# A recurrence of 30 steps on one core: eps inside the aggregated variance, another set of groups transposed by DMA, one PSUM copy moved to VectorE, and a new order of work inside a slot

## The chip, the cores and the metric

The kernel runs on one core of a Trainium2 chip. The metric is the device time of one launch in microseconds (us). Engine names are those of the profile: PE is TensorE (PEld its weight loads), DVE is VectorE, ACT is ScalarE, POOL is GpSimd, SP is SyncE, which here only issues DMAs.

## The reference, cut to what matters

The network has two layers over 3327 nodes with 256 features: a graph attention and a mixture of experts, then a second graph attention and a recurrent feed-forward part. Only that last part, the recurrence, is touched. It computes, 30 times in a row and row by row:

```python
def step(h, _):
    h = h + 0.01 * jnp.tanh(h)
    h = h * jax.nn.sigmoid(h)
    h = _layernorm(h, ln_w, ln_b)          # (h - mu) * rsqrt(var + 1e-5) * w + bias
    h = jnp.einsum('bsc,dc->bsd', h, W) + b
    return (h, None)
x, _ = jax.lax.scan(step, x, None, length=30)
```

It starts from a layernorm of `x`, and its result is added to `x`. Every row is independent of the others, so the steps of different rows can run beside each other.

## The kernel before, in words

The rows lie as 26 tiles of 128 rows in the on-chip tensor `x` (128 partitions x 26 x 256, float32). The recurrence works on seven *groups*: groups 0 to 5 have four tiles each, group 6 has two. A group in a step is one `Group` object, numbered `at` from 0 to 209; `at % 7` is the group, `at // 7` the step. The state is kept times 100 (`S`), and the subtraction of the mean and the weights of the normalization are folded into the 256 x 256 matrix `wc` and the row `bb`, so only the reciprocal standard deviation is needed for each row, and it is applied after the product.

One group in one step goes through these pieces, with their lines in the kernel before:

- `tanh` (L1109, ACT) writes `th`; `add` (L1112, POOL) adds the state to it; `silu` (L1116, ACT) writes `z`.
- `measure` (DVE): for each tile `bn_stats` over 256 values (L1121), which leaves six numbers [...], then `bn_aggr` (L1124), which makes mean and variance of them, then one small instruction that adds eps (L1127). `invert` (L1132, POOL) raises it to the power -1/2.
- The product needs `z` transposed. A group that is not `away` is turned on the core: `turn_here` issues two PE transposes of 128x128 per tile (L1142), and ACT copies them out of PSUM for two tiles at a time (L1144). A group that is `away` is turned by DMA: `send_away` lets ACT split the 4-byte values into 2-byte halves (L1152, once for two tiles) and SP issue a store of them to DRAM (L1154); `take_back` lets SP issue transposing DMAs that bring them back (L1164, one for two tiles). `AWAY` (L1091) lists the groups that are turned by DMA, from `at` = 2 on.
- `product` (L1177, PE): two matmuls per tile with `wc`, each of which the profile records as two. `evict` (L1187, DVE): one instruction per tile multiplies by the reciprocal deviation, adds `bb` and writes the state. In the last step it also loads the kept `x` (`old`, L1194, SP), adds it (L1195, DVE) and stores the result (L77, SP).

The loop at L1209 is the schedule. In each pass, a *slot*, it issues pieces of seven different groups: `tanh` for the group six ahead of the product, `add` and `silu` five ahead, `send_away` four ahead, `measure` and the turning three ahead, `invert` one ahead, the product, and the eviction of the group one behind. Nearly all of these are bound to that order on their engine (`keep_in_program_order`), so each engine's queue is the order of the lines in the loop: on ACT the split copies, then `tanh`, `silu` and the copies out of PSUM; on DVE the eviction, then `measure`; on POOL `invert`, then `add`; on PE the product, then the transposes; on SP the sends, then the eviction's DMAs in the last step, then the takes. The engines wait for each other only where data or a buffer demands it. Buffers: three `th`, four `z`, two `zT`, two product tiles in PSUM, three tiles for the halves and five for what comes back, four places in DRAM.

The matmuls of the second attention (L286) run until about 1080 us; the first steps of the recurrence are begun beside them.

Of the kernel before, what the change touches and what calls it, by code (L numbers as in the profile page):

```python
# [11 lines left out]
F32 = mybir.dt.float32  # L12
# [5 lines left out]
ALU = mybir.AluOpType  # L18
# [3 lines left out]
P = 128  # L22
ALPHA = 0.2
EPS = 1e-5
N_STEPS = 30
S = 100.0
G = 4
# [4 lines left out]
def gat_moe_gat_recurrent_ffn(ctx: ExitStack, tc: tile.TileContext, a: dict, out: bass.AP):  # L32
    nc = tc.nc
    N, D = a["x"].shape
# [65 lines left out]
    neg_half = const.tile([P, MOST], F32, name="neg_half")  # L100
# [902 lines left out]
        for name, bufs in (("th", 3), ("z", 4), ("zT", 2))  # L1003
    }
    narrow = ctx.enter_context(tc.tile_pool(name="narrow", bufs=8))
    ps = ctx.enter_context(tc.tile_pool(name="ps2", bufs=2, space=PSUM))
    with ExitStack() as st:
        keep = st.enter_context(tc.tile_pool(name="keep2", bufs=1))
# [71 lines left out]
    with ExitStack() as st:  # L1080
# [7 lines left out]
        spaces = [space[:, i * G * D : (i + 1) * G * D] for i in range(8)]  # L1088
        room_parts, room_back = cycle(spaces[:3]), cycle(spaces[3:])

        AWAY = (0, 1, 3, 5)  # L1091
        COUNT = len(groups)
        LAST = N_STEPS * COUNT

        class Group:

            def __init__(self, at):
# [3 lines left out]
                self.hs = x[:, self.ts[0] : self.ts[0] + self.n, :]  # L1101
                self.away = at % COUNT in AWAY and at > 1

# [12 lines left out]
                self.put(nc.scalar.activation(self.z, self.th, AF.Silu, scale=1.0 / S))  # L1116

            def measure(self):
                stats = narrow.tile([P, G, 6], F32, name="stats")
                for j in range(self.n):  # L1120
                    self.put(nc.vector.bn_stats(stats[:, j, :], self.z[:, j, :]))  # L1121
                self.v = narrow.tile([P, G, 2], F32, name="v")
                for j in range(self.n):
                    self.put(nc.vector.bn_aggr(self.v[:, j, :], stats[:, j, :]))  # L1124
                self.r = narrow.tile([P, G], F32, name="rr")
                self.put(
                    nc.vector.tensor_scalar(self.r[:, : self.n], self.v[:, : self.n, 1], EPS, None, op0=ALU.add)  # L1127
                )

            def invert(self):  # L1130
                r = self.r[:, : self.n]
                self.put(nc.gpsimd.tensor_tensor(r, r, neg_half[:, : self.n], ALU.pow))  # L1132

            def turn_here(self):
                pool = next(turns)
                zT = steps["zT"].tile([P, G, KD, P], F32, name="zT")
                for c in range(self.n // 2):
                    pt = pool.tile([P, 2, KD, P], F32, name="bank")
                    for j in range(2):
                        for k in range(KD):  # L1140
                            (tc.keep_in_program_order if self.at > 1 else lambda ins: ins)(
                                nc.tensor.transpose(pt[:, j, k, :], self.z[:, 2 * c + j, k * P : (k + 1) * P], ident)  # L1142
                            )
                    self.put(nc.scalar.copy(zT[:, 2 * c : 2 * c + 2, :, :], pt))  # L1144
                self.zT = lambda j, k: zT[:, j, k, :]

            def send_away(self):
# [52 lines left out]
        live = {}  # L1200

        def on(at, *what):
            if 0 <= at < LAST:
                if at not in live:
                    live[at] = Group(at)
                for w in what:
                    w(live[at])

        for at in range(-6, LAST + 2):  # L1209
            on(at + 4, lambda g: g.away and g.send_away())  # L1210
            on(at - 1, Group.evict)
            live.pop(at - 1, None)
            on(at + 6, Group.tanh)
            on(at + 1, Group.invert)
            on(at + 5, Group.add)
            on(at + 3, Group.measure)
            on(at, Group.product)
            on(at + 3, lambda g: g.away and g.take_back())
            on(at + 5, Group.silu)
            on(at + 3, lambda g: g.away or g.turn_here())  # L1220


# [47 lines left out]
```

## Time and profile before

| | |
|---|---|
| median of 3 runs | 1831.34 us (1829.67 to 1831.44) |
| the profiled execution | 1831.93 us |
| its span, first to last instruction | 1830.2 us |
| mean granted TensorE clock | 0.996 |
| the recurrence's products (L1177) | from 1083.0 to 1822.4 us |
| busy in the span | PE 1778.3, DVE 1318.7, ACT 1229.7, POOL 914.0 us |
| costliest groups of the recurrence (us busy, mean ns of one) | products on DMA-turned tiles 422.2, 379; products on PE-turned tiles 281.0, 379; `add` 464.8, 2213; evictions 325.0, 477; `bn_stats` 274.0, 411; split copies 235.2, 1044; `tanh` 209.1, 996; `silu` 207.1, 986; `invert` 206.7, 984 |
| issued by DMA | 236 stores `apart<-adjT` of 256 KB, 236 transposes `adjT<-apart` |

How to read it: times of one instruction overlap the next one on the same engine, so the mean length of a matmul is not what it takes of PE's stream; for that the starts of neighbours are compared. A view of the profile names an instruction by its line and by the tensor it writes and reads (`po<-wc,adjT` is a product on what the DMA brought back, since those buffers share the memory of the adjacency matrix `adjT`). The profiled execution's own time stands beside its span because a sum of durations belongs to that execution, not to the median.

### The profile page before, as it was taken

To read this page: it belongs to the slowest core of one execution; us is meant where nothing else is said; L and a number is where in the kernel's file an instruction comes from. 1 tells how busy PE (TensorE), PEld (TensorE's weight loads), DVE (VectorE), ACT (ScalarE), POOL (GpSimd) and SP (SyncE) were. 2 spreads that over 40 slices of the span, in tenths; PEclk is the share of its full clock that TensorE was granted. 3 is DMA by queue.
4 is the path that set the end of the run, shared out by engine and by line. 5 is a ranking of instruction groups with operands and counts; after the bars stand their busy time and mean duration, and the time that the engine had idled before them with its cause. 6 is when DMAs were issued, how large, how long until landed. Compare 5 with 4: busy or idle time off the path is not lost.

```text
span 1830.2 us, 32461 instructions
## 1 busy us (share of the span) xinstructions
PE 1778.3 (97%) x10896; PEld 1622.7 (89%) x10896; DVE 1318.7 (72%) x4039; ACT 1229.7 (67%) x1587; POOL 914.0 (50%) x702
## 2 busy tenths in 40 slices
PE   6999999999999999799999999999999999999998
PEld 6999999898999999688888878888888888888887
DVE  6888888853222222657676679999999999999998
ACT  2877667642122121456666579999999999999994
POOL 3011212155454542101111028898889889888984
PEclk9999999999999999899999999999999999999999
DMA  8897360257696876400000037777777777767777
GB/s 174 119 125 85 73 102 15 67 168 207 218 264 186 220 203 164 154 15 16 18 22 14 12 91 175 175 166 175 167 168 179 168 177 168 173 166 169 179 168 224
DMA packets 454531, 252.98 MB, mean 138 GB/s; under 512 B 327493, under 2 KB 426620, under 8 KB 454362
## 3 DMA queue, kind: packets, MB, share of 16 engines
q1 hardware_dynamic: 436226, 212.51, 47.1%
q0 software_dynamic: 13456, 33.60, 10.8%
q10 hardware_dynamic: 4680, 4.76, 0.8%
q8 instruction: 89, 1.46, 0.3%
q14 instruction: 80, 0.66, 0.1%
HBM read 168.19 MB, written 97.20 MB: 145 GB/s over the span
## 4 chain that ended last, share of the span: by engine, by line
PE 54%; DVE 4%; DMA 1%; issue 0%; ACT 0%; POOL 0%; SPq 0%; ACTq 0%; DVEq 0%; POOLq 0%
PE po L1177 35%; PE acc L286 14%; PE bank L1142 4%; DVE pT L281 1%; PE acc L163 1%; DMA old<-kept 1%; DVE x L1187 0%; DVE x L1027 0%; DVE stats L1121 0%; DMA given<-wh,to 0%; DVE x L1195 0%; DMA zT<-given 0%; DVE st L116 0%; POOL rstd L121 0%; DVE low L1061 0%
## 5 line engine op out<-in xcount | busy, mean ns | idle before, releaser
L276 ACT ACTIVATE e<-rb,minus,full 128x384 f32<-128x384 f32 (+3 forms) x494 | 399.2, 823 | 168.0 <-DVE pT L281 147.1
L1112 POOL TENSOR_TENSOR th<-th,x 128x1024 f32<-128x1024 f32 (+1 forms) x210 | 464.8, 2213 | 94.3 <-ACT th L1109 86.6
L281 DVE SCALAR_TENSOR_TENSOR pT<-e,part,adjT 128x384 f32<-128x384 f32 (+3 forms) x494 | 383.4, 782 | 118.3 <-PE acc L286 102.3
L1177 PE MATMUL po<-wc,adjT 128*128 128x256 f32 x1888 | 422.2, 379 | 0.0
L1177 PEld LDWEIGHTS po<-wc,adjT 128*128 128x128 f32 x1888 | 356.4, 190 | 47.6 <-DVE x L1187 0.3
L1187 DVE SCALAR_TENSOR_TENSOR x<-po,rr,bb 128x256 f32<-128x256 f32 x780 | 325.0, 477 | 61.6 <-PE po L1177 61.1
L286 PE MATMUL acc<-wh,pT 128*128 128x129 f32 x2704 | 310.7, 276 | 2.1 <-DVE pT L281 2.1
L286 PEld LDWEIGHTS acc<-wh,pT 128*128 128x128 f32 x2704 | 305.4, 192 | 3.2 <-DVE pT L281 2.5
L286 PE MATMUL acc<-s_wh,pT 128*128 128x257 f32 x1352 | 295.5, 381 | 4.0 <-DVE pT L281 4.0
L286 PEld LDWEIGHTS acc<-s_wh,pT 128*128 128x128 f32 x1352 | 255.8, 190 | 43.1 <-DVE pT L281 7.4
L1177 PE MATMUL po<-wc,zT 128*128 128x256 f32 x1232 | 281.0, 379 | 0.6 <-DVE x L1187 0.6
L1121 DVE BATCH_NORM_STATS2 stats<-z 128x6 f32<-128x256 f32 x780 | 274.0, 411 | 1.4 <-ACT z L1116 1.4
L1177 PEld LDWEIGHTS po<-wc,zT 128*128 128x128 f32 x1232 | 229.2, 190 | 29.6 <-issue 0.9
L1152 ACT COPY adjT<-z 128x1024 int16<-128x1024 int16 x236 | 235.2, 1044 | 4.8 <-DVE pT L281 2.0
L121 POOL TENSOR_TENSOR rstd<-ve,neg_half 128x4 f32<-128x4 f32 (+3 forms) x28 | 31.9, 1141 | 411.5 <-DVE ve L119 313.0
L1109 ACT ACTIVATE th<-x 128x1024 f32<-128x1024 f32 (+1 forms) x210 | 209.1, 996 | 28.9 <-DVE x L1187 23.8
L1132 POOL TENSOR_TENSOR rr<-rr,neg_half 128x4 f32<-128x4 f32 (+1 forms) x210 | 206.7, 984 | 26.4 <-DVE rr L1127 26.3
L1116 ACT ACTIVATE z<-th 128x1024 f32<-128x1024 f32 (+1 forms) x210 | 207.1, 986 | 8.3 <-POOL th L1112 2.3
L931 ACT ACTIVATE e<-bank 128x512 f32<-128x512 f32 x61 | 36.4, 597 | 241.0 <-issue 183.2
L939 DVE TENSOR_TENSOR pT<-e,bank 128x512 f32<-128x512 f32 x61 | 41.9, 687 | 190.8 <-PE bank L881 160.7
L903 POOL DMA_INDIRECT given<-wh,to x61 | 61.1, 1001 | 119.2 <-DVE wh L902 102.8
L594 POOL DMA_INDIRECT lists<-pair,ati x52 | 63.5, 1221 | 107.5 <-DVE ati L581 49.3
(202 smaller groups left out, 1731.9 us busy)
## 6 DMA issues: line engine op xcount, KB each, us to landing
wh<-in_w_dram SPq DMA_DIRECT2D x120, 512.0 KB
apart<-adjT SPq DMA_DIRECT2D x236, 256.0 KB
first_set<-in_w_dram SPq DMA_DIRECT2D x63, 512.0 KB
in_bytes<-in_adj_dram POOLq DMA_DIRECT2D x3, 2496.0 KB
asked<-e POOLq DMA_DIRECT2D x42, 128.0 KB
adjT<-apart SPq DMA_TRANSPOSE x236
x<-in_x_dram SPq DMA_DIRECT2D x6, 512.0 KB
kept<-x SPq DMA_DIRECT2D x8, 384.0 KB
```

What stands on the lines that cost most here:

```text
L276: nc.scalar.activation(e[:, : n * P], rb[:, : n * P], AF.Relu, scale=sc.full[:, j, h : h + 1], bias=sc.minus[:, j, h : h + 1],)
L281: masked = nc.vector.scalar_tensor_tensor(pT[:, : n * P], e[:, : n * P], sc.part[:, j, h : h + 1], adjT[:, j // 2, ts[0] * P : (ts[-1] + 1 ...
L286: nc.tensor.matmul(po[c], lhsT=pT[:, c * P : (c + 1) * P], rhs=wh[:, j, h, :], start=(j == 0 and c % per_bank == 0), stop=(j == NT - 1), s ...
L1109: self.put(nc.scalar.activation(self.th, self.hs, AF.Tanh, scale=1.0 / S))
L1112: self.put(nc.gpsimd.tensor_tensor(self.th, self.th, self.hs, ALU.add))
L1116: self.put(nc.scalar.activation(self.z, self.th, AF.Silu, scale=1.0 / S))
L1121: self.put(nc.vector.bn_stats(stats[:, j, :], self.z[:, j, :]))
L1132: self.put(nc.gpsimd.tensor_tensor(r, r, neg_half[:, : self.n], ALU.pow))
L1142: nc.tensor.transpose(pt[:, j, k, :], self.z[:, 2 * c + j, k * P : (k + 1) * P], ident)
L1152: self.put(nc.scalar.copy(parts[:, c : c + 2], halves[:, c : c + 2]))
L1177: nc.tensor.matmul(self.po[:, j, :], lhsT=self.zT(j, k), rhs=wc[:, k, :], start=(k == 0), stop=(k == KD - 1),)
L1187: nc.vector.scalar_tensor_tensor(self.hs[:, j, :], self.po[:, j, :], self.r[:, j : j + 1], bb, op0=ALU.mult, op1=ALU.add)
```

## The change

The change does four things in the recurrence.

1. **eps.** The statistics of eight groups get one tensor that is written once, `measures`, with nine numbers for each tile: the six of `bn_stats` and a third entry that is constant (count 0, mean 0, sum of squares EPS x 256). `bn_aggr` reads all nine, so its variance contains eps. The DVE instruction that added eps is gone, and POOL's power reads the aggregated variance directly.
2. **Which groups are turned by DMA.** `AWAY` is (0, 2, 4, 5, 6) instead of (0, 1, 3, 5): 18 tiles instead of 16. On PE remain groups 1 and 3 instead of 2, 4 and 6: 8 tiles instead of 10. Groups 4, 5, 6 and the next step's 0 follow each other.
3. **One copy out of PSUM.** Of group 3's two copies, the first is done by DVE instead of ACT.
4. **The order of a slot.** `tanh` and `invert` come ahead of `send_away`. The eviction belongs to the product's own group and stands behind the product and ahead of `measure`, where it was of the group one behind and stood near the head. The loop ends two passes earlier, and the number of pieces is the same.

On the queues that means: ACT has `tanh` before the split copies; DVE has the eviction of group s before `measure` of s+3 where it had `measure` of s+4 after it; on SP, in the last step, the eviction's load and store of group s stand ahead of the take of s+3, where those of s-1 did. POOL's and PE's order within a slot is the same.

```diff
+    measures = ctx.enter_context(tc.tile_pool(name="measures", bufs=1)).tile([P, 8, G, 9], F32, name="stats")
+    nc.vector.memset(measures[:, :, :, 6:8], 0.0)
+    nc.vector.memset(measures[:, :, :, 8:9], EPS * D)
...
-        AWAY = (0, 1, 3, 5)
+        AWAY = (0, 2, 4, 5, 6)
...
             def measure(self):
-                stats = narrow.tile([P, G, 6], F32, name="stats")
+                stats = measures[:, self.at % 8]
                 for j in range(self.n):
-                    self.put(nc.vector.bn_stats(stats[:, j, :], self.z[:, j, :]))
+                    self.put(nc.vector.bn_stats(stats[:, j, :6], self.z[:, j, :]))
                 self.v = narrow.tile([P, G, 2], F32, name="v")
                 for j in range(self.n):
                     self.put(nc.vector.bn_aggr(self.v[:, j, :], stats[:, j, :]))
+
+            def invert(self):
                 self.r = narrow.tile([P, G], F32, name="rr")
                 self.put(
-                    nc.vector.tensor_scalar(self.r[:, : self.n], self.v[:, : self.n, 1], EPS, None, op0=ALU.add)
-                )
-
-            def invert(self):
-                r = self.r[:, : self.n]
-                self.put(nc.gpsimd.tensor_tensor(r, r, neg_half[:, : self.n], ALU.pow))
+                    nc.gpsimd.tensor_tensor(
+                        self.r[:, : self.n], self.v[:, : self.n, 1], neg_half[:, : self.n], ALU.pow
+                    )
+                )
...
-                    self.put(nc.scalar.copy(zT[:, 2 * c : 2 * c + 2, :, :], pt))
+                    copied = nc.vector.tensor_copy if (self.at % COUNT, c) == (3, 0) else nc.scalar.copy
+                    self.put(copied(zT[:, 2 * c : 2 * c + 2, :, :], pt))
...
-        for at in range(-6, LAST + 2):
-            on(at + 4, lambda g: g.away and g.send_away())
-            on(at - 1, Group.evict)
-            live.pop(at - 1, None)
+        for at in range(-6, LAST):
             on(at + 6, Group.tanh)
             on(at + 1, Group.invert)
+            on(at + 4, lambda g: g.away and g.send_away())
             on(at + 5, Group.add)
+            on(at, Group.product, Group.evict)
             on(at + 3, Group.measure)
-            on(at, Group.product)
             on(at + 3, lambda g: g.away and g.take_back())
             on(at + 5, Group.silu)
             on(at + 3, lambda g: g.away or g.turn_here())
+            live.pop(at, None)
```

## The prediction

> **What bounds the kernel now.** I read the slices first, then the stages, the waits and the order of time. In the page's totals and its 40 slices (one digit is the busy tenth of a slice) the part that the diff touches, the recurrence, is the last 40%:
>
> ```profile
> PE 1778.3 (97%) x10896; PEld 1622.7 (89%) x10896; DVE 1318.7 (72%) x4039; ACT 1229.7 (67%) x1587; POOL 914.0 (50%) x702
> ...
> PE   6999999999999999799999999999999999999998
> ```
>
> All engines look busy there, so the view by stages (us; then PE, PEld, DVE, ACT, POOL, clock, DMA share, GB/s) and the waits from 1050 us on decide:
>
> ```profile
> 1400.00:1600.00 200.00, 200.00 (x1009) 176.97 (x1009) 181.91 (x693) 189.10 (x220) 178.32 (x114) 1.00 0.76 172
> ```
> ```profile
> POOL th L1112 <- ACT th L1109: 78.8, 61, 2.9
> DVE x L1187 <- PE po L1177: 61.1, 89, 1.8
> ...
> ACT th L1109 <- DVE x L1187: 23.8, 29, 0.8
> ...
> PE po L1177 <- DVE x L1187: 0.6, 1, 0.6
> ```
>
> DVE waits for PE, ACT for DVE, POOL for ACT; PE waits 0.6 us in all. The chain starts at PE. The order of time gives PE's prices and the slack of the DMA path (start, length):
>
> ```profile
> 1501.84 7.07 PE L1177 MATMUL po<-wc,adjT 128*128 128x256 f32 x32
> ...
> 1508.75 1.04 PE L1142 MATMUL bank<-ident,z 128*128 128x128 f32 x8
> ...
> 1509.62 3.62 PE L1177 MATMUL po<-wc,zT 128*128 128x256 f32 x16
> ...
> 1512.96 1.99 ACT L1152 COPY adjT<-z 128x1024 int16<-128x1024 int16 x2
> ...
> 1513.35 1.66 DVE L1187 SCALAR_TENSOR_TENSOR x<-po,rr,bb 128x256 f32<-128x256 f32 x4 [0.88 <-PE po L1177]
> 1514.03 6.01 SPq L1154 DMA_DIRECT2D apart<-adjT  x4
> ...
> 1515.04 1.06 ACT L1109 ACTIVATE th<-x 128x1024 f32<-128x1024 f32 x1
> ...
> 1520.13 5.31 SPq L1164 DMA_TRANSPOSE adjT<-apart  x4
> ...
> 1526.48 3.83 PE L1177 MATMUL po<-wc,adjT 128*128 128x256 f32 x17
> ```
>
> 16 product records cost (7.07-3.62) = 3.45 us, so 0.2156 us each from start to start; 8 transposes cost 1509.62-1508.75 = 0.87, so 0.109 each. A step has 104 records and 20 transposes: 22.42 + 2.18 = 24.60 us, and the trace's step (group 0 from 1501.84 to 1526.48) is 24.64. **PE issues without a gap: a step is the sum of its matmuls.**
>
> [...] busy is 100%, weight loads are 177 of 200 us, and only the start-to-start times show that nothing is left. [...] Here its row says 273, but it takes 109 of PE's stream, which is the price used. [...] `take_back` waits on the landing of `send_away`, with everything behind it in SP's queue; the trace shows it, in SP's own waits from 1400 to 1600 us:
>
> ```profile
> SPq L1164 <- DMA apart<-adjT: 18.9, 16, 2.2
> ```
>
> **The change, part by part.** P0 to P6 are the products of groups 0 to 6 (P6 half as long), "turn" the transposes on PE.
>
> *Groups turned by DMA.* Before, groups 2, 4, 6 (10 tiles, 20 transposes a step) stay on PE; after, 1 and 3 (8 tiles, 16). In all 600+16 transposes become 480+8, 128 fewer. A step falls by 4 x 0.109 = 0.44 to 24.20 us. Before the first product, group 2's eight go (16 transposes stand at 1081.23, the product at 1083.00): 0.87. So up to the last step: 0.87 + 29 x 0.436 = **13.5 us less**, if PE stays without gaps.
>
> *ACT.* One int16 copy a step more (nine for eight, 0.95 from start to start), two PSUM copies fewer (five become four, one goes to DVE; 0.47 each): about 0. ACT stays at 189.1/200 x 24.64 = 23.3 us, now of 24.2.
>
> *DVE.* Seven eps additions go (172 ns rows): -1.2 us. One PSUM copy comes: between ACT's 576 ns row and the 687 of the DVE row with a PSUM operand of that size (L939), I take 0.66. `bn_aggr` on nine entries for six is not in the trace: between 0 and half of its 66 ns step, 0 to 0.9 us; I take 0.1. Net -0.4 of 22.4: off the path. The copy sits in the slot of P0, 3.45 + 0.87 = 4.33 long, where DVE has 3.24 + 0.66 = 3.9; without that cover it costs at most 0.6. Two memsets at the layer's start run while DVE is idle.
>
> *The order of a slot.* Eviction of s still precedes `tanh` of s+7, but three waits are new or longer.
> (a) On ACT, `tanh` now stands ahead of the copies. Above, the copies of group 0 ran at 1512.96, before the `tanh` that had to wait for the eviction's end at 1515.01; they would now start at 1516.0, 3 us later, with silu, PSUM copy and SP's send behind them.
> (b) On DVE, `measure` of s+3 now follows the eviction of s. So POOL's power of s+3, which stands ahead of the addition of s+7, waits for `bn_aggr`, some 3.3 us after the eviction starts. POOL has 0.99 + 2.32 = 3.3 us of work in a slot of 3.45, so it keeps up; the addition comes 1.5 to 2 us later than `tanh` would allow.
> (c) On SP, groups 4, 5, 6, 0 go in a row. From P0 = 0 (P4 14.7, P5 18.1, P6 22.5, next P0 24.2), with evictions starting 0.28 after a product and ending 1.66 later, sends come at about 4.2/5.2 (group 4), 8.4/9.4 (5), 12.2 (6), 15.2/16.2 (0), 22.1/23.1 (2). Takes follow, each behind the next group's send: 9.7, 12.6, 16.5, 17.8, 25.0. A take of two transposes needs 2 x 1.25 us on SP, and I give 2.6 us from a transpose's issue to its landing (packets of the pair issued from 1503.82 end near 1507.9). First halves land at 12.3, 15.2, 19.1, 20.7, 27.6: 2.4, 2.9, 3.4, 3.5 and 4.4 us ahead of their products. Before, by the same rule, the nearest was group 0: 1520.13 + 2.6, 3.8 ahead of its product at 1526.48. Thinner now, but positive, so I cost it at nothing. SP issues 9 x (0.37+1.25) = 14.6 us a step (13.0 before); DMA share goes from 0.76 to 0.76 x 9/8 x 24.64/24.20 = 0.87.
>
> *The ends.* The head shows no new stall: the send of group 2 comes before the last attention result, and its second take, behind the last `kept` store, lands near 1087, before P2 at about 1090. The tail is not PE's alone:
>
> ```profile
> 1808.87 0.38 SPq L77 DMA_DIRECT2D out_dram<-x  x1
> 1809.35 3.12 SPq L1164 DMA_TRANSPOSE adjT<-apart  x2
> ...
> 1812.52 0.57 SPq L1194 DMA_DIRECT2D old<-kept  x1
> ```
>
> In the last step each take stands behind a store that waits for DVE. After the change three groups (4, 5, 6) come back there instead of one, each behind the store of the group three ahead, not four. From the last P0 to the span's end the trace has 1830.2-1797.5 = 32.7 us; the same walk, with an `old` load landing in 3.5 us, gives P4 and P5 about 1 us late and an end near 33.7. I take **+1.0**, between -2.5 (the shorter tail on PE wins) and +4 (takes wait for contended stores).
>
> **Sum**: -0.87 - 12.64 + 1.0 = -12.5 us. The profiled execution took 1831.93 (span 1830.2): 1819.4. The median, 1831.34, stands 0.59 lower: **1818.8**.
>
> **Rivals.** A. *As summed* (76%): own range 1815.3 to 1821.8, from the tail's bounds.
> B. *Another engine takes the bound* (11%). ACT has 0.9 us a step free and now waits for the eviction at the head of each slot. Losing 0.25 of the 0.44 us on most steps (29 x 0.25 = 7) leaves about -5: 1826. For it: ACT's 23.3 us and 4.7 us slots (tanh, two copies, silu, PSUM copies) against PE's 4.33. Against it: the next slot has no copy and gives the time back.
> C. *Nothing measurable* (5%): the lateness of (a) and (b) eats the 0.44 whole: about 1831. Within 0.2% (3.7 us) the measurement can't tell it from no change.
> D. *Slower* (8%). The burst 4, 5, 6, 0 overruns SP. One group costs there two transposes plus 0.75 of sends, against 3.45 a slot. At 1.25 us each there is room. [...] a mean of 1.9 builds 3.5 x (3.8+0.75-3.45) = 3.8 us of backlog against some 2.7 of slack: PE waits 1.1, 32 us in 29 steps, so +19 in all: 1851. It decides from about 1.8 us. Against: before's four takes in a row took 5.31 us, 1.33 each.
> That the transposes don't fall as counted is excluded by the instruction streams of both kernels: 616 and 488.
>
> **How the numbers follow.** Faster by over 0.2%: A and B, 87%; same 5%; slower 8%. The range 1815.3 to 1827 holds A nearly whole and half of B, and leaves out C and D.
>
> **What would show it.** Right: 488 transposes at 0.109; a step of 24.20 us; PE's share still 100% from 1200 to 1750; waits of POOL's power on `bn_aggr` new, PE's waits still near zero; the last product about 12 us earlier. Wrong: PE idle before products of groups 4, 5, 0 on a DMA landing (D, and the slack is mis-sized), before transposes on silu (B, C), or a last step longer than 37 us (the tail).

## The result, and the profile after

The changed kernel takes 1825.56 us (median; 1820.76 to 1828.77) against 1831.65 for the kernel before in the same session: a ratio of 0.9964, 95% interval 0.9954 to 0.9975. That is 6.1 us faster by the medians (6.6 by the ratio), where 12.5 were forecast. Its profiled execution took 1820.76 us (span 1819.0), 11.2 less than that of before, and 4.9 of that lie in stages which the change does not touch: the second attention ended at 1074.5 us instead of 1079.4. Without them the two profiles differ by 6.3, about as much as the medians (6.1).

First the page's totals and its slices, then the same 200 us by stages (us; PE, PEld, DVE, ACT, POOL, granted clock, DMA share, GB/s):

```profile
PE 1764.8 (97%) x10768; PEld 1608.8 (88%) x10768; DVE 1303.0 (72%) x3861; ACT 1214.2 (67%) x1557; POOL 916.2 (50%) x702
...
PE   6999999999999999799999999999999999999997
```
```profile
1400.00:1600.00 200.00, 200.00 (x991) 176.97 (x990) 180.53 (x652) 187.55 (x215) 181.66 (x116) 1.00 0.85 195
```

There are 128 matrix instructions fewer, as counted. PE is still busy for all of the stage, DVE and ACT have each a little more room than before, and the DMA engines are at 0.85. The order of time on PE shows one whole step:

```profile
1500.47 3.62 PE L1181 MATMUL po<-wc,zT 128*128 128x256 f32 x16
1503.92 7.07 PE L1181 MATMUL po<-wc,adjT 128*128 128x256 f32 x32
1510.83 1.04 PE L1145 MATMUL bank<-ident,z 128*128 128x128 f32 x8
1511.70 5.35 PE L1181 MATMUL po<-wc,adjT 128*128 128x256 f32 x24
1516.89 1.04 PE L1145 MATMUL bank<-ident,z 128*128 128x128 f32 x8
1517.76 3.62 PE L1181 MATMUL po<-wc,zT 128*128 128x256 f32 x16
1521.22 3.62 PE L1181 MATMUL po<-wc,adjT 128*128 128x256 f32 x16
1524.67 2.54 PE L1181 MATMUL po<-wc,zT 128*128 128x256 f32 x11
```

From group 3's product at 1500.47 to the next at 1524.67 are 24.20 us, with 16 transposes where there were 20. The waits of the whole recurrence, from 1050 us on:

```profile
POOL rr L1132 <- DVE v L1127: 73.5, 92, 4.8
DVE x L1191 <- PE po L1181: 72.8, 173, 1.8
...
ACT th L1112 <- DVE x L1191: 37.7, 58, 1.2
...
PE po L1181 <- DMA adjT<-apart: 5.5, 2, 4.0
DVE x L1199 <- DMA old<-kept: 5.5, 3, 2.2
```

The first line is new and expected: POOL's power now waits for `bn_aggr`. The last two are what the sum did not hold. They lie in the last step alone, which grew from 32.73 us (from the start of the last P0, group 0's product, to the span's end) to 39.43. Its order of time, cut to SP, PE and the final addition (L1199):

```profile
1792.82 2.87 SPq L1168 DMA_TRANSPOSE adjT<-apart  x2
...
1796.38 0.46 SPq L1198 DMA_DIRECT2D old<-kept  x1
1796.73 3.69 PE L1181 MATMUL po<-wc,adjT 128*128 128x256 f32 x16 [1.90 <-DVE x L1199]
1796.93 0.51 SPq L77 DMA_DIRECT2D out_dram<-x  x1
1797.55 5.57 SPq L1168 DMA_TRANSPOSE adjT<-apart  x2
...
1801.99 1.23 DVE L1199 SCALAR_TENSOR_TENSOR x<-x,old 128x1024 f32<-128x1024 f32 x1 [2.12 <-DMA old<-kept]
...
1804.40 2.21 SPq L1168 DMA_TRANSPOSE adjT<-apart  x1
1804.46 5.38 PE L1181 MATMUL po<-wc,adjT 128*128 128x256 f32 x16 [4.04 <-DMA adjT<-apart]
...
1811.34 1.97 PE L1181 MATMUL po<-wc,adjT 128*128 128x256 f32 x8 [1.50 <-DMA adjT<-apart]
```

PE waits before group 4, group 5 and group 6, the three that now come back by DMA. The take of group 5 holds SP for 5.57 us where a pair takes 2.6 in the steady part; right before it a load of `old` and a store of `out` were issued. The first bracket names DVE, but that is not what ended the wait: DVE's addition is nothing that this product reads, and the eviction that frees its buffer (group 2's) had ended at 1795.46. By the semaphore updates in the trace, the first half of group 4's take landed at 1796.59, 0.14 us before the product. Groups 5 and 6 too start 0.14 us behind the landing of their takes.

The difference, term by term, from the two profiled executions (us):

| term | forecast | measured |
|---|---|---|
| head, end of the attention to the first product | -0.87 | -0.85 |
| 29 steps | -12.64 | -12.13 |
| last step | +1.0 (-2.5 to +4) | +6.7 |
| sum | -12.5 | -6.3 |

### The profile page after: what moved, and what is told of

Read it like the earlier page. It is cut to its first block, busy times and chain, and to the rows that moved or that the text cites. A ratio compares the mean times of both kernels' runs of the same rounds, so it can differ in the third digit from the quotient of the medians.

```text
span 1819.0 us, 32184 instructions
## 1 busy us (share of the span) xinstructions
PE 1764.8 (97%) x10768; PEld 1608.8 (88%) x10768; DVE 1303.0 (72%) x3861; ACT 1214.2 (67%) x1557; POOL 916.2 (50%) x702
## 3 DMA queue, kind: packets, MB, share of 16 engines
q0 software_dynamic: 13456, 33.60, 10.7%
## 4 chain that ended last, share of the span: by engine, by line
PE 54%; DVE 3%; DMA 1%; issue 0%; ACT 0%; SPq 0%; POOL 0%; ACTq 0%; DVEq 0%; POOLq 0%
PE po L1181 36%; PE acc L286 15%; PE bank L1145 3%; DVE pT L281 1%; PE acc L163 1%; DMA old<-kept 1%; DVE x L1030 0%; DMA given<-wh,to 0%; DMA zT<-given 0%; DVE x L1199 0%; DVE x L1191 0%; DVE st L116 0%; POOL rstd L121 0%; DVE low L1064 0%; SPq L1168 0%
## 5 line engine op out<-in xcount | busy, mean ns | idle before, releaser
L1181 PE MATMUL po<-wc,adjT 128*128 128x256 f32 x2144 | 480.0, 380 | 7.5 <-DMA adjT<-apart 5.5
L1181 PEld LDWEIGHTS po<-wc,adjT 128*128 128x128 f32 x2144 | 405.9, 191 | 63.5 <-issue 4.9
L1156 ACT COPY adjT<-z 128x1024 int16<-128x1024 int16 x268 | 266.9, 1039 | 2.1 <-DVE pT L281 2.0
L1132 POOL TENSOR_TENSOR rr<-v,neg_half 128x4 f32<-128x4 f32 (+1 forms) x210 | 205.6, 979 | 94.2 <-DVE v L1127 88.9
L1181 PE MATMUL po<-wc,zT 128*128 128x256 f32 x976 | 220.8, 379 | 0.1
L1181 PEld LDWEIGHTS po<-wc,zT 128*128 128x128 f32 x976 | 182.9, 190 | 24.0 <-DVE x L1191 0.5
```

What stands on the lines that cost most here:

```text
L1132: nc.gpsimd.tensor_tensor(self.r[:, : self.n], self.v[:, : self.n, 1], neg_half[:, : self.n], ALU.pow)
L1156: self.put(nc.scalar.copy(parts[:, c : c + 2], halves[:, c : c + 2]))
L1181: nc.tensor.matmul(self.po[:, j, :], lhsT=self.zT(j, k), rhs=wc[:, k, :], start=(k == 0), stop=(k == KD - 1),)
```

## The experiments

"Step" is the mean of the 28 steps between the first and the last. All ratios are against runs of the kernel before on the same chip, and all times of steps are from one profile of each kernel.

| kernel | ratio, 95% interval | first step | step | last step |
|---|---|---|---|---|
| before | 1 | 24.64 | 24.64 | 32.73 |
| changed | 0.9964 [0.9954, 0.9975] | 24.50 | 24.21 | 39.43 |
| away_alone | 1.0000 [0.9987, 1.0012] | 26.70 | 24.29 | 41.84 |
| order_and_eps_alone | 1.0049 [1.0035, 1.0063] | 24.64 | 24.76 | 39.27 |
| take_before_store | 0.9974 [0.9961, 0.9986] | 24.20 | 24.21 | 41.09 |
| last_step_on_pe | 0.9930 [0.9916, 0.9944] | 24.20 | 24.21 | 33.60 |
| ends_after_the_loop | one run, no measure | 24.20 | 24.20 | (39.76) |
| old_early | 0.9949 [0.9936, 0.9962] | 24.25 | 24.29 | 34.76 |
| old_early_last_step_on_pe | 0.9947 [0.9934, 0.9960] | 24.20 | 24.31 | 33.20 |
| old_early_take_first | 0.9929 [0.9916, 0.9943] | 24.20 | 24.27 | 32.24 |
| eps_and_copy_undone | 0.9977 [0.9970, 0.9984] | 24.51 | 24.27 | 39.90 |
| away_and_eps | 0.9980 [0.9971, 0.9989] | 24.20 | 24.24 | 41.97 |
| away_eps_last_step_on_pe | 0.9932 [0.9918, 0.9946] | 24.20 | 24.24 | 32.16 |

### Where the lost 6 us went

**last_step_on_pe** takes the three takes out of the last step and pays 20 transposes for them:

```diff
-                self.away = at % COUNT in AWAY and at > 1
+                self.away = at % COUNT in AWAY and 1 < at < LAST - 3
```

> The changed kernel, but groups 4, 5 and 6 of the last step are turned on PE (20 transposes more, 2.2 us, and 5 copies out of PSUM on ScalarE). No take is left in the last step. T: last step 33 to 35 us, 10 to 12 us faster than before. R: last step near 40 us; if loads of old alone set the tail, about 36 us.

Measured: 0.9930 (10.4 us faster than before by the medians, 12.8 by the ratio), last step 33.60. The forecast gain is there as soon as the last step has no takes. This version beats both kernels.

**take_before_store** changes SP's order there: a group's load, final addition and store are issued behind the take of the group three ahead. On DVE the final addition moves with them, behind `measure` of that group.

```diff
             def evict(self):
...
+            def finish(self):
+                ts, n = self.ts, self.n
                 if self.at >= LAST - COUNT:
...
             on(at + 3, lambda g: g.away and g.take_back())
+            on(at, Group.finish)
```

> The changed kernel, but in the last step the load of old, its addition and the store of a group are issued after the take of the group three ahead instead of before it. Nothing else moves. T: PE no longer waits some 2, 4 and 1.7 us for landings, last step 33 to 36 us, in all 10 to 12 us faster than before. R (or: the takes are late because the DMA engines are full, whatever the order on SP): last step stays at 38 to 40 us, 6 us faster than before.

Measured: last step 41.09. The wait before group 4 is gone, and group 5's product starts 22.3 us after P0 instead of 24.9: its take was issued 3.2 us earlier, though the pair held SP for 6.27 us and its first half needed 7.4 us to land instead of 6.8. Group 6 loses what was gained:

```profile
1808.90 1.22 DVE L1202 SCALAR_TENSOR_TENSOR x<-x,old 128x1024 f32<-128x1024 f32 x1 [6.43 <-DMA old<-kept]
1810.04 1.65 DVE L1191 SCALAR_TENSOR_TENSOR x<-po,rr,bb 128x256 f32<-128x256 f32 x4
...
1811.75 3.78 PE L1181 MATMUL po<-wc,adjT 128*128 128x256 f32 x8 [3.64 <-DVE x L1191]
```

Its take had landed at 1806.08. But there are two product buffers, and the one that it needs is freed by group 4's eviction (1810.04), which stands on DVE behind a final addition that waited 6.43 us for its `old` load. So SP's order alone is not the cause: a late load holds PE up on a second way, through DVE.

**ends_after_the_loop** moves the loads, final additions and stores of the last step behind the last product, so the takes are alone with the sends.

```diff
+        ended = []
         for at in range(-6, LAST):
...
+            if at >= LAST - COUNT:
+                ended.append(live[at])
             live.pop(at, None)
+        for g in ended:
+            g.finish()
```

> The last step's loads of old, final additions and stores are moved behind the last product; the takes of groups 4, 5 and 6 are alone on SP and on the DMA engines. From the last P0 to the last product P6 the changed kernel needed 31.7 us. Theory 'loads and stores hold up the takes': 22.5 to 23.5 us, PE without a wait of over 0.5 us, and each pair of transposes holds SP 2.5 to 3.2 us. Rival 'the new slot order or the burst of takes itself is late': P6 at 26 us or later, with PE waiting for landings. The span's end comes later than in the changed kernel in either case (seven adds and stores in a row), so the total is no measure here.

The order of time of its last step, on PE (last P0 at 1781.39, inside the first line):

```profile
1780.75 4.26 PE L1181 MATMUL po<-wc,adjT 128*128 128x256 f32 x19
1784.85 1.04 PE L1145 MATMUL bank<-ident,z 128*128 128x128 f32 x8
1785.72 3.62 PE L1181 MATMUL po<-wc,zT 128*128 128x256 f32 x16
1789.18 3.62 PE L1181 MATMUL po<-wc,adjT 128*128 128x256 f32 x16
1792.63 3.62 PE L1181 MATMUL po<-wc,zT 128*128 128x256 f32 x16
1796.08 8.80 PE L1181 MATMUL po<-wc,adjT 128*128 128x256 f32 x40
```

The last line is groups 4, 5 and 6 in one run of 40 records: not one wait, and the last product starts 21.6 us after P0 instead of 31.72. This is better than the 22.5 to 23.5 expected, although one pair of takes held SP for 3.6 us, more than the expected 3.2. So neither the new order nor the burst of takes is late by itself; the loads, final additions and stores of the last step make them late.

**old_early** separates loads from stores. The loads of `old` are issued in steps 20 to 26, one group a step, into unused memory:

```diff
+            if 0 <= at < LAST and at // COUNT == 20 + at % COUNT:
+                ts = groups[at % COUNT]
+                here = slice(ts[0] * P, (ts[-1] + 1) * P)
+                tc.keep_in_program_order(
+                    nc.sync.dma_start(
+                        olds[at % COUNT][:, : len(ts), :], kept[here, :].rearrange("(t p) d -> p t d", p=P)
+                    )
+                )
```

> The changed kernel, but the seven loads of old are issued in steps 20 to 26, one group a step, into unused memory; in the last step only takes and stores stand on SP. Theory 'the loads are what holds up the end' (by DMA engines shared with the takes, and by DVE waiting for them, which makes the stores and with them the takes behind them late): last step 33 to 35 us instead of 39.4, about 5 us faster than the changed kernel, near 1820.5. Rival 'the takes behind the stores are late whatever the loads do': last step 37 to 39, at most 2 us faster. The steps 20 to 26 stay at 24.2 to 24.4 us.

Measured: last step 34.76, so moving the loads brings back 4.7 of the lost time. The total gained less than that, since three of the steps with a load took 25.17, 24.56 and 25.19 us: there too a load of 512 KB made PE wait for takes (1.6 us in three waits between 1600 and 1665 us of old_early_last_step_on_pe, which has the same loads). The last step still has two waits of PE, 2.16 us before group 4 and 1.70 us before group 6 (L1182 and L1169 are this kernel's product and take):

```profile
1797.15 0.37 SPq L77 DMA_DIRECT2D out_dram<-x  x1
1797.63 2.87 SPq L1169 DMA_TRANSPOSE adjT<-apart  x2
...
1801.63 8.83 PE L1182 MATMUL po<-wc,adjT 128*128 128x256 f32 x32 [2.00 <-DVE x L1198]
...
1805.97 0.38 SPq L77 DMA_DIRECT2D out_dram<-x  x1
1806.45 2.82 SPq L1169 DMA_TRANSPOSE adjT<-apart  x1
...
1812.00 1.97 PE L1182 MATMUL po<-wc,adjT 128*128 128x256 f32 x8 [1.54 <-DMA adjT<-apart]
```

Each of these takes is issued right behind a store that had waited for DVE, and each product starts 0.14 us behind the landing of its take.

**old_early_take_first** puts `finish` behind the take, as in take_before_store, with the loads already done.

> old_early with the final addition and the store of a group issued behind the take of the group three ahead. In old_early PE still waited 2.16 us before group 5's and 1.70 us before group 6's product, and the takes of both were issued 0.1 us behind a store that had waited for DVE. Theory 'what is left is SP's order': these waits fall below 0.5 us each, last step 31 to 33 us instead of 34.8, 2 to 3 us faster than old_early. Rival 'what is left is the store sharing the DMA engines with the takes': last step stays at 34 to 36 us. take_before_store, the same move with the loads in place, gained nothing (last step 41.1).

Measured: last step 32.24, 2.5 us shorter than old_early, and 0.9929 (12.1 us faster than before by the medians, 13.0 by the ratio). So once the loads are away, the order is worth 2.5 us: SP's, and with it DVE's, which were not tried apart. PE's waits did not all go. The expectation names the wrong group for the first one: it stood before group 4. That one and the one before group 6 are gone, and a wait of 2.35 us before group 5 is new. There the pair of takes started at 1795.36, 0.6 us behind a send and 1.1 behind a store, held SP for 4.87 us, and its first half landed at 1801.53, 6.2 us after its issue, with no load in flight. Both theories hold a part, and the missing gain of take_before_store fits: there the same order also brought group 5 forward, and the load took the gain away again.

**old_early_last_step_on_pe** has both remedies.

> Both remedies: loads of old early, and groups 4, 5 and 6 of the last step turned on PE. If they remove the same loss (takes held up), this is no more than 0.5 to 1.5 us faster than turning on PE alone, last step 32 to 33.5 us, near 1817.5. If the loads cost by themselves at the end (the last DVE addition waiting for its load) it is 2 us or more faster than that, last step 31 us.

Measured: last step 33.20, as expected of two remedies for one loss. The total is 0.9947, about 3 us behind last_step_on_pe and not ahead of it, though the intervals overlap: two of the steps with a load took 25.3 us. The expectation had left that price out.

### What the parts of the change do

**away_alone** is the kernel before with the new set of groups and nothing else.

```diff
-        AWAY = (0, 1, 3, 5)
+        AWAY = (0, 2, 4, 5, 6)
```

> The kernel before with AWAY (0, 2, 4, 5, 6) and nothing else changed. Theory T (the lost gain is in the last step: takes of groups 4, 5 and 6 stand on SP behind the stores of the result and share the DMA engines with them and with the loads of old): the step is 24.20 us if the other three edits are not needed for it; in the last step a take stands behind the store of the group four ahead, one more than in the changed kernel, so the last step is between, about 35 to 37 us against 32.7 and 39.4; in all -13.5 + 2 to 4, about 10 us faster than before. Rival R (the new order of a slot makes the last step late by itself, through the power that waits for bn_aggr): last step at 33 us, some 13 us faster. If the other edits are needed to hold the shorter step (ACT's PSUM copies, the eps addition on DVE), the step is 24.3 to 24.6 and PE shows gaps in every step.

Measured: no gain at all in the total. The last step took 41.84, the first 26.70, and most others 24.3. A miss: the set alone shortens the 29 steps by 7.6 us (706.9 against 714.5) instead of 12.6, and the last step gives that back. The order of time from 1102 to 1108 us, cut to POOL's addition, the eps addition (L1127), the eviction between them and the late product, shows why:

```profile
1102.42 2.34 POOL L1112 TENSOR_TENSOR th<-th,x 128x1024 f32<-128x1024 f32 x1 [1.70 <-ACT th L1109]
...
1103.07 1.72 DVE L1127 TENSOR_SCALAR rr<-v 128x4 f32<-128x4 f32 x1
...
1104.71 1.25 DVE L1187 SCALAR_TENSOR_TENSOR x<-po,rr,bb 128x256 f32<-128x256 f32 x3
...
1106.02 2.21 PE L1177 MATMUL po<-wc,adjT 128*128 128x256 f32 x9 [2.34 <-DVE x L1187]
```

The addition of four numbers a row took 1.72 us instead of 0.17, and ended at 1104.79, 30 ns after POOL's addition (1102.42 + 2.34). So it was with all 87 of the 210 eps additions that took over 0.4 us: each ended 24 to 36 ns after an addition on POOL, 65.5 us of DVE more in all. (27 more began in the last 0.12 us of an addition and took their usual 0.17.) DVE was then busy 198.0 of 200 us from 1400 to 1600, evictions came late, and PE waited (2.34 us in the rows above). In the kernel before, only two eps additions met POOL's addition in this way (they took 1.32 and 0.46 us). The traces show the delay and its end; they do not show what in the two engines causes it.

**away_and_eps** adds only the eps edit to away_alone (`measures`, `bn_aggr` on nine entries, POOL's power from the variance, as in the diff of the change).

> The kernel before with the changed set of groups and with eps inside the aggregation; slot order and PSUM copies as before. It differs from away_alone only in that the eps addition on DVE is gone. In away_alone 87 of the 210 eps additions took over 0.4 us (172 ns otherwise), up to 2.1 us, and each of these ended 24 to 36 ns after the end of an addition on POOL: 65 us of DVE in all. Theory 'the eps addition is blocked while POOL adds': the first step falls from 26.7 to 24.2 to 24.5 us and the later steps from 24.32 to 24.20, together about 5 us, so near 1824 if the last step stays at 40 to 42 us. Rival 'the old slot order is what is late with fewer transposes on PE': steps stay at 24.3 and the first at 26 or more, no more than 1 us faster than away_alone.

Measured: first step 24.20, most later ones 24.20, and the ratio 0.9980: 3.7 us faster than away_alone, 4.1 by the two profiles (2.5 in the first step, 1.6 in the next 28). The rival, that the old slot order is late with fewer transposes, falls. The last step is again 42 us; PE waits 8.2 us in it, and DVE 8.9 for two loads issued together. This is the way through DVE again, since the take of the waiting product, group 5's, had landed at 1799.69:

```profile
1798.44 1.12 SPq L1197 DMA_DIRECT2D old<-kept  x2
1803.09 1.23 DVE L1198 SCALAR_TENSOR_TENSOR x<-x,old 128x1024 f32<-128x1024 f32 x1 [8.85 <-DMA old<-kept]
...
1806.81 8.35 PE L1180 MATMUL po<-wc,adjT 128*128 128x256 f32 x24 [8.06 <-DVE x L1190]
```

**away_eps_last_step_on_pe** is that with the last step of last_step_on_pe (the same line).

> The same with groups 4, 5 and 6 of the last step turned on PE, so that the tail is as short as in last_step_on_pe; it differs from that kernel in slot order and in group 3's copy alone. If the slot order and the copy are worth nothing by themselves once eps is folded in: within 1.5 us of last_step_on_pe (ratio 0.993), step 24.20, last step 33 to 34 us. If the new order is needed: steps of 24.3 or more or a last step of 36 or more, 3 us or more slower than that.

Measured: 0.9932 against 0.9930. With eps folded in and no takes in the last step, the new slot order and the DVE copy bring nothing that can be measured (each interval reaches 2.6 us to either side). With takes in the last step it is 2.5 us shorter with them (39.43 in the changed kernel, 41.97 in away_and_eps).

**eps_and_copy_undone** is the reverse: the changed kernel with the eps addition as an instruction of its own and both copies on ACT.

```diff
-                    copied = nc.vector.tensor_copy if (self.at % COUNT, c) == (3, 0) else nc.scalar.copy
-                    self.put(copied(zT[:, 2 * c : 2 * c + 2, :, :], pt))
+                    self.put(nc.scalar.copy(zT[:, 2 * c : 2 * c + 2, :, :], pt))
```

> The changed kernel with the eps addition back on DVE as an own instruction and both PSUM copies of group 3 on ACT; groups and slot order as changed. Theory of the prediction (DVE and ACT lie beside PE, so these two edits are worth nothing by themselves): step 24.20 us, median within 1.5 us of the changed kernel. Rival (the edits were needed to fit the shorter step, because a copy on ACT behind tanh is late or DVE has no room): step 24.3 to 24.6 us, 3 to 10 us slower, with PE waiting on ACT's copy before group 3's product or before a transpose.

Measured: most steps 24.20, with a few bumps up to 25.04; 57 of the eps additions were held up in this way, 46.7 us in all. The bumps are not DVE's: each stands before the product of a group 4, 5 or 6 whose take had landed 0.14 us earlier. The ratio is 0.9977 against 0.9964, some 2 us worse, and the intervals overlap. Between the two expectations: DVE absorbs these 46.7 us in the new order. The two edits were not tried apart here.

**order_and_eps_alone** is the changed kernel with the old set of groups, (0, 1, 3, 5).

> The changed kernel with AWAY back at (0, 1, 3, 5); group 3 is then turned by DMA, so the copy on VectorE does not occur. T: step 24.64 us as before, the one take in the last step (group 5) now behind the store of the group three ahead: last step 33 to 35 us, in all 0 to 2 us slower than before. R: last step near 39 us, 6 us slower.

Measured: 9 us slower than before by the ratio, 10 by the medians, more than either theory said. The last step is 39.27 with only group 5 among the last three coming back by DMA: its take was issued at 1820.55, right behind a store at 1820.06, and PE waited 5.3 us. So the rival holds a part: with this order a take in the last step stands behind a later store. The steps of 24.76 come from small gaps on PE, of up to 0.4 us. By the semaphore updates in the trace they stand before the products of groups 0 and 1, which start 0.14 us behind the landing of their takes: with this order the takes of the old set have no lead left in the steady part either.

## Why the prediction was right, and where it failed

- **PE's stream as the bound**: right. A step is the sum of its records, 24.64 and 24.20 us, and in the changed kernel too eight transposes take 0.87 us of the stream (1510.83 to 1511.70), though the row of one lasts 0.27; the 29 steps gave 12.13 of 12.64 us, the rest being three early steps of 24.36 to 24.50, in each of which PE waited for a take of group 5 or 6 that landed late. The head gave 0.85 of 0.87.
- **ACT and DVE off the path**: right in the changed kernel. The copy on DVE takes 0.65 us (0.66 forecast, the author's estimate), four `bn_aggr` on nine entries 0.39 instead of 0.36. But the eps edit was costed wrongly. The prediction took off seven additions at 172 ns, and did not ask what they would cost in the new alternation. With the new groups they meet POOL's additions, and that price, shown by away_alone and away_and_eps, is about 4 us in the old order; in the new order no wait of PE was traced to it.
- **Takes ahead of their products**: right in sign for the steady part, and mis-sized. The prediction gave a transpose 2.6 us from issue to landing; by the semaphore updates it needs 3.5 (median of the steady part, 3.1 to 5.3). The first halves of groups 4, 5, 6, 0 and 2 therefore land 1.3, 1.3, 1.6, 1.8 and 3.4 us ahead of their products (medians), where 2.4, 2.9, 3.4, 3.5 and 4.4 were forecast. (The 20.7 among the forecast landings should be 20.4 by its own rule; that changes nothing.) About 1 us was left, and it was enough: ends_after_the_loop shows the burst 4, 5, 6 without a wait of PE, so rival D's price was never reached. Its 1.9 us for an issue was the author's estimate; in the changed kernel the median of the steady part is 1.25. Rival B gave the number that came out (1826) by a mechanism that did not occur: PE waited for no other compute engine in the steady part.
- **The tail**: this step failed, in size. The forecast was +1.0, at most +4, and it measured +6.7. The walk gave an `old` load 3.5 us to land and a take 2.6 us, and left about 1 us of lateness. In the last step DVE got group 3's load 5.6 us after the issue (1796.38 to 1801.99), the first halves of the takes of groups 4, 5 and 6 landed 3.8, 6.8 and 6.8 us after theirs, and the pair of group 5 held SP 5.57 us. The last product came 10.1 us later than in ends_after_the_loop (31.72 against 21.6 after P0): waits of 2.1, 4.2 and 1.7 us before groups 4, 5 and 6, 1.7 us because PE slowed down after the longest of them (0.427 us a record instead of 0.216, at a granted clock of 0.51), and 0.3 us before group 3 for an eviction. Against the kernel before (22.98) it came 8.7 us later, and 2.0 of them came back, since the end followed the last product more closely. The upper bound, +4, named takes that wait for contended stores; it left out the loads, and that three groups in a row would each wait. The sign that the prediction gave for this, a last step longer than 37 us, is what the trace showed.

A better price for a load stood in the trace of the kernel before: the one issued at 1812.52, which the prediction shows, was waited for until 1817.52, 5.0 us later:

```profile
1817.52 1.22 DVE L1195 SCALAR_TENSOR_TENSOR x<-x,old 128x1024 f32<-128x1024 f32 x1 [1.41 <-DMA old<-kept]
```

The range, 1815.3 to 1827, held the 1825.56, and that was luck: the own range of the case that was summed ends at 1821.8, and the rest was room for half of rival B. The sum was off by one term. last_step_on_pe and old_early_take_first, with most of that term taken out, gain 10.4 and 12.1 us by the medians, 12.8 and 13.0 by the ratios.

## What to carry to other kernels

A change that is right for the steady part should be walked through the last pass on its own, with the durations of that pass: there the transfers that end the work share the issuing queue and the DMA engines with those that feed PE (from 1776 us on in the changed kernel, one hardware queue carried 15585 of 15587 packets and filled 87.7% of the 16 engines' time). A lead of about 1 us, enough in every steady step but three here, was no reserve for that pass, where first halves landed 3.8 to 6.8 us after the issue instead of 3.5. When more groups depend on a transfer, a way that needs none may be better for the last few, even if it costs PE more: here a last step of 33.60 us instead of 39.43. And before a small DVE instruction is costed at its usual duration, see whether GpSimd will be at work beside it after the change: the 0.17 us here became up to 2.13.

## What the runs showed of the hardware that was not expected

- In away_alone, a DVE addition of 172 ns (L1127) took up to 2.13 us when it began during POOL's addition `th<-th,x`, and ended 24 to 36 ns after it (87 of 210). The final addition of the last step (1.22 us) was held up too: in the changed kernel one took 2.27 us, begun 0.09 us into such an addition of 1.28 us, and ended 1.1 us after it.
- A transposing DMA pair holds SP for 2.6 us in the steady part and for up to 6.27 us when a load and a store of 512 KB are in flight (take_before_store). Its first half lands 3.5 us after the issue in the steady part, 7.4 us there, and 6.2 us in old_early_take_first, where a store and a send but no load stood before it.
- In the changed kernel, PE waited 4.2 us for group 5, ran 1.3 us at its usual pace, and then took 0.427 us instead of 0.216 from start to start for seven records, between 1805.7 and 1809.0 us; so the 16 records took 5.38 instead of 3.62 us. The granted clock of just this stretch is 0.51, and 1.00 in the steady part; it was 0.50 from 1805.5 to 1808.9 us, so for 3.4 us. After 8.2 us of waiting in away_and_eps it was twelve records, and there the slow pace began at once (24 records in 8.35 us, where 24 take 5.35 in the steady part). No shortest wait can be read from these traces: after 2.16 us in old_early PE slowed down (32 records in 8.83 us instead of 7.07), after 2.1 us in the changed kernel (16 in 3.69 us) and 2.5 us in away_alone (the first nine in 2.21 us) it did not.
